# Restoring the node order of a row of attention scores with a VectorE transpose of 32x32 squares before the row goes to DRAM

## The chip, the cores and the metric

The kernel runs on one core of a Trainium2 chip. The metric is the device time of one execution in microseconds (us), the median of several runs; lower is better. The core's engines are TensorE (PE: matmuls; PEld: its weight loads), VectorE (DVE), ScalarE (ACT), GpSimd (POOL) and SyncE (SP), whose queue issues most of the DMA transfers. Each engine works through its own instructions in a fixed order and waits on semaphores for the others.

## The reference

There are 32 graphs of 512 nodes with 256 features. Each graph goes through four layers of graph attention; every layer normalises `x`, applies a ReLU, computes attention and adds the result to `x`. Layers 1 and 2 form their attention from one score per node on each side. Cut to what matters here (`B` = 32, `N` = 512):

```python
def layer_1(h, adj, W, a):                     # layer 2 is alike, with exp(-leaky_relu(.))
    Wh = h @ W.T
    src = Wh @ a[:256, 0]                      # a score for each row of the attention
    dst = Wh @ a[256:, 0]                      # a score for each column
    e = src[:, :, None] + dst[:, None, :]
    e = jnp.where(e > 0, e, 0.2 * e)           # leaky ReLU
    e = jnp.where(adj > 0, e, NEG_INF)
    return softmax(e) @ Wh

for layer in (0, 1, 2, 3):
    h = relu(layernorm(x))
    x = x + gnn[layer](h, adj)
```

Layer 0 uses dot products of the nodes, two tanh convolutions and a softmax, layer 3 a bilinear score with a leaky ReLU. The output is `x` after layer 3, as float32.

## The kernel before, in words

The work is done one graph at a time, with up to five graphs in flight (`FLIGHT = 5`, five "slots"), and for each graph in tiles of 128 nodes (`NT` = 4 tiles). Attention is kept transposed: partitions hold the columns' nodes (128 of them per tile `c`), the free dimension holds all 512 rows.

The order of instructions is made when the program is built. Each operation is registered by `op(engine, cost, after, emit, *tiles)`: `cost` is a pair of nanoseconds, how long the engine is held and when the result is there. `Plan.best` runs a list scheduler over all operations of all graphs with these prices, tries several spacings between graphs, keeps the shortest plan, and the instructions are written out in that order. The buffers (36 pages of SBUF, 8 PSUM banks, 4 value buffers, 5 slots) are handed out by this plan too. The prices are constants near the top: `A_PRELU`, `A_PRELU2`, `A_EXP` for ScalarE, `V_TINY`, `V_MASK` for VectorE, `D_OUT`, `D_SPREAD`, `D_TURN` for DMA transfers.

For layers 1 and 2 `scored_values` multiplies the nodes with a weight matrix that has two more columns (L596), so that each bank holds 256 values and two scores per node. VectorE copies the two scores of each tile into a small tile `sd` (L600), whose partition is the node within its tile and whose free dimension is the tile's number; ScalarE copies the values (L603).

`leaky_exp_t` then needs one of the two scores as a row of 512 that is the same on all 128 partitions. It has two ways. The first five and the last five graphs (`turned`) use TensorE: four transposes of a broadcast column (L619) put the row into a PSUM bank, `bank_r`. The other 22 graphs go through DRAM: `collect` (L624) writes the 128x4 scores to DRAM, partition after partition, and `spread` (L628) reads the 512 numbers back onto every partition, into the tile `row`. In this row the numbers stand in the order partition, tile; the node order is tile, partition. ScalarE therefore reads `row` with a step of four floats when it adds the other score and takes the leaky ReLU (`leaky`, L635, activation function Prelu). The exp follows (`exp`, L639), then VectorE applies the adjacency mask (L764 in layer 1, L791 in layer 2), and `attend` (L662) multiplies the attention with the values.

Other lines that are spoken of later: in layer 0, ScalarE's exp (L700), VectorE's mask (L703), the reciprocal of the softmax sum on VectorE (L711) and the tanh on ScalarE (`y`, L714), which reads an attention bank and so sets it free; in layer 3, the leaky ReLU (L924), the same activation function on consecutive floats in SBUF. The weights are loaded at the start by transfers that GpSimd issues (L289), after a few memsets.

Of the kernel before, what the change touches and what calls it, by code (L numbers as in the profile page):

```python
# [11 lines left out]
F32 = mybir.dt.float32  # L12
# [3 lines left out]
AF = mybir.ActivationFunctionType  # L16
# [3 lines left out]
P = 128  # L20
EPS = 1e-5
ALPHA = 0.2
# [17 lines left out]
A_COPY, A_HALF, A_PRELU, A_EXP, A_TANH = (477.0, 597.0), (253.0, 373.0), (570.0, 693.0), (519.0, 640.0), (373.0, 474.0)  # L40
A_BIAS, A_PRELU2 = (570.0, 687.0), (629.0, 722.0)
# [2 lines left out]
A_HALF_BIAS = (345.0, 460.0)  # L44
A_NORM, A_JOIN, V_SPLIT = (491.0, 590.0), (620.0, 767.0), (332.0, 422.0)
D_TURN = (1310.0, 2600.0)
D_OUT, D_SPREAD = (550.0, 3500.0), (550.0, 4500.0)
D_X, D_ADJ, D_ADJ0 = (550.0, 5000.0), (550.0, 12000.0), (550.0, 2500.0)
G_LOAD = (800.0, 5000.0)

# [108 lines left out]
def kernel(  # L159
# [31 lines left out]
    nc = tc.nc  # L191
    B, N, H = x.shape
    NT = N // P
    HC = H // P
    HALF = H // 2
    FLIGHT = 5
    PAGES, VALUES = 36, 4
    LEAD = 2

    const = ctx.enter_context(tc.tile_pool(name="const", bufs=1))  # L200
    work = ctx.enter_context(tc.tile_pool(name="work", bufs=1))
    ps = ctx.enter_context(tc.tile_pool(name="ps", bufs=1, space=PSUM))
    dram = ctx.enter_context(tc.tile_pool(name="dram", bufs=2, space=bass.MemoryType.DRAM))


    cols, pair, stat, turned = [P, HC, N], [P, NT, H], [P, NT], [P, NT, N]
# [8 lines left out]
        "code": (turned, BF16, "code"), "adj": (turned, I32, "adj"),  # L215
        "planes": ([P, 2, H], U16, "planes"), "planesT": ([P, 2 * HC, P], U16, "planesT"),
        "bank": ([P, 512], F32, "bank"), "v": (None, F32, "v"),
        "st": ([P, NT, 6], F32, None), "mv": ([P, NT, 2], F32, None), "sd": ([P, 2, NT], F32, None),
        "ve": (stat, F32, None), "rstd": (stat, F32, None), "rs": (stat, F32, None), "off": (stat, F32, None),
        "top": (stat, BF16, None),  # L220
    }
    POOLS = {"page": PAGES, "v": VALUES, "code": 1, "adj": 1, "planes": 3, "planesT": 2, "bank": 8,
             "slot": FLIGHT, "ahead": FLIGHT + 1}

    plan = Plan()
# [1 line left out]
    class Tiles:  # L227
# [10 lines left out]
        def place(self, key):  # L238
            if key not in self.places:
                self.places[key] = plan.place(key if key in POOLS else KINDS[self.kind(key)][2])  # L240
            return self.places[key]
# [22 lines left out]
    ident = const.tile([P, P], F32, tag="ident", name="ident")  # L264
# [72 lines left out]
    def seven_of(w, dst, half, after, *keys):  # L337


        def blocks():  # L340
# [29 lines left out]
    a = [load(l1_sb, rows_of(l1_w), "raw0")]  # L370
# [4 lines left out]
    a = [load(l2_aug[:, :, :H], rows_of(l2_w))]  # L375
    a = ready["l2"] = a + transposed(lambda: l2_aug[:, :, :H], l2_wt, a, "raw1")
    a = a + [load_column(l2_ac, l2_a.rearrange("o n -> (o n)"))]
# [3 lines left out]
    t = transposed(l3_sb, wt3, [load(l3_sb, rows_of(l3_w), "raw2")], "raw2", "raw4")  # L381
    a = product(lambda d: awt()[:, d, :], a12_sb, lambda c: wt3()[:, c, :], H,
                t + [load(a12_sb, rows_of(l3_a12), "raw3")], "raw3", "raw4", "raw5")
    a = product(lambda d: m3_sb()[:, d, :], wt3, lambda c: awt()[:, c, :], H, a, "raw4", "raw5", "raw6")
# [4 lines left out]
    a = [load(lambda i=i: l3_wide()[:, :, i * (HALF + 1) : i * (HALF + 1) + HALF],  # L389
              rows_of(l3_w2)[:, :, i * HALF : (i + 1) * HALF], "raw8") for i in range(2)]  # L390
# [8 lines left out]
    for i in range(VALUES):  # L399
        v = const.tile([P, NT, LEAD + H + 1], F32, tag=f"v{i}", name=f"v{i}")  # L400
        nc.gpsimd.memset(v[:, :, LEAD + H :], 1.0)
        v_bufs.append(v)


    def graph(b, adj_before, x_before):


        T = Tiles(b)

        def op(engine, cost, after, emit, *keys):  # L410
            return plan.op(engine, cost, after, emit, b, T.uses(keys))
# [10 lines left out]
        def e(l, c):  # L422

            return T[f"e{l}_{c // 2}"][:, c % 2, :]
# [20 lines left out]
        coded, code = [], None  # L445
        for g in range(NT // 2):
            code = op("V", V_CODE, [got_adj[2 * g + 2], code], partial(classes, g), "adj", "code", "slot")
# [107 lines left out]
        def block_sums(dst, source, b, after, left):  # L555
# [24 lines left out]
            else:  # L580
# [2 lines left out]
            return (lambda x: [sums[x][0]] if x in sums else list(after),  # L583
                    lambda x: d(sums[x][1]) if x in sums else b(*plain[x]))

        def scored_values(l, hs, w_aug, ready):


            cols = w_aug.shape[2]
            vs, ss = [], []  # L590
            for t in range(NT):
                key = f"bank_v{l}{t}"

                def product(t, key):
                    for c in range(HC):
                        nc.tensor.matmul(T[key][:, :cols], T[f"hT{l}"][:, c, t * P : (t + 1) * P],  # L596
                                         w_aug[:, c, :], start=(c == 0), stop=(c == HC - 1))

                def scores(t, key):
                    nc.vector.tensor_copy(T[f"sd{l}"][:, : cols - H, t], T[key][:, H:cols])  # L600

                def values(t, key):
                    nc.scalar.copy(T[f"v{l}"][:, t, LEAD : LEAD + H], T[key][:, :H])  # L603

                a = op("PE", pe(n256=4), [hs[t]] + ready, partial(product, t, key), key, f"hT{l}")
                ss.append(op("V", V_TINY, [a], partial(scores, t, key), key))
                vs.append(op("A", A_HALF, [a], partial(values, t, key), key, f"v{l}"))
            return vs, ss

        def leaky_exp_t(l, ss, sign):  # L610

            turned = b < FLIGHT or b >= B - FLIGHT
            key = f"bank_r{l}" if turned else f"row{l}"
            line = []

            def turn(t):
                nc.tensor.transpose(T[key][:, t * P : (t + 1) * P],  # L619
                                    T[f"sd{l}"][:, 0, t : t + 1].to_broadcast([P, P]), ident)  # L620

            def collect():
                line.append(dram.tile([P, NT], F32, tag=f"row_{T.places['slot']['number']}", name=f"row{l}_{b}"))
                nc.sync.dma_start(out=line[0], in_=T[f"sd{l}"][:, 0, :])  # L624

            def spread():
                d = line[0]
                nc.sync.dma_start(out=T[key][:, 0, :], in_=bass.AP(tensor=d.tensor, offset=d.offset, ap=[[0, P], [1, N]]))  # L628

            def leaky(c):  # L630
                if turned:
                    row = T[key].rearrange("q (t p) -> q t p", t=NT)
                else:
                    row = T[key][:, 0, :].rearrange("q (p t) -> q t p", t=NT)
                nc.scalar.activation(e(l, c).rearrange("q (t p) -> q t p", t=NT), row, AF.Prelu,  # L635
                                     bias=T[f"sd{l}"][:, 1, c : c + 1], alpha=ALPHA)

            def exp(c):
                nc.scalar.activation(e(l, c), e(l, c), AF.Exp, scale=sign)  # L639

            a = None
            if turned:
                for t in range(NT):
                    a = op("PE", pe(nt=1), [ss[t], a], partial(turn, t), key)
            else:
                a = op("D", D_OUT, ss, collect)
                a = op("D", D_SPREAD, [a], spread, key)
            ls = [op("A", A_PRELU, [a], partial(leaky, c), key, f"e{l}_{c // 2}") for c in range(NT)]
            return [op("A", A_EXP, [x], partial(exp, c), f"e{l}_{c // 2}") for c, x in enumerate(ls)]

        def attend(l, es, vs, use):
# [23 lines left out]
        for g in range(NT // 2):  # L675
            key = f"bank_v0{g}"
# [11 lines left out]
            a = op("PE", pe(n256=8), hs[two(g)], partial(values, g, key), key, "hT0")  # L688
            vs += [op("V", V_ADD, [a], partial(biased_v, g, j, key), key, "v0") for j in range(2)]
        es = []  # L690
        for c in range(NT):
            key = f"bank_q{c}"
# [12 lines left out]
            a = op("PE", pe(n512=4), qs, partial(similar, c, key), key, "hT0", "fa0")  # L705
            a = op("A", A_COPY, [a], partial(exp0, c, key), key, f"e0_{c // 2}")
# [22 lines left out]
        a = None  # L729
        for c in range(NT):  # L730
            a = op("PE", pe(n512=4), [ys[c], a], partial(again, c), "bank_z0", "bank_z1", "y0", f"e0_{c // 2}")
        zs = [op("A", A_COPY, [a], partial(evacuate_z, k), f"bank_z{k}", "zT") for k in range(HC)]
        xs = []
        for g in range(NT // 2):
            key = f"bank_o{g}"
# [18 lines left out]
            a = op("PE", pe(n256=8), zs + ready["w1"], partial(second_conv, g, key), key, "zT")  # L754
            bs = [op("V", V_PSUM, [a] + ready["b1"], partial(biased, 2 * g + j, key), key, "z0") for j in range(2)]
            a = op("A", A_EXP, bs, partial(tanh2, g), "z0")
# [11 lines left out]
        vs, ss = scored_values(1, hs, l1_aug, ready["l1"])  # L768
# [18 lines left out]
        vs, ss = scored_values(2, hs, l2_aug, ready["l2"])  # L787
# [109 lines left out]
        ls = [(sb[c // 2, 0], sb[c // 2, 1]) for c in range(NT)]  # L897
# [35 lines left out]
        a = op("V", (334.0, 425.0), hi, highest, "crest3")  # L933
        a = op("D", D_TURN, [a], partial(turn, 0, 2), "crest3")
        a = op("V", (900.0, 1000.0), [a], tops, "crest3")
        a = op("D", D_TURN, [a], partial(turn, 1, 0), "crest3")
        row = op("A", A_PRELU2, [a], leaky_row, "crest3")
        ls = [op("A", A_PRELU2, [a, hi[c // 2]], partial(leaky3, c), f"e3_{c // 2}") for c, a in enumerate(ls)]
        ls = [op("V", V_MASK, [a, row], partial(shifted, c), "crest3", f"e3_{c // 2}") for c, a in enumerate(ls)]
# [41 lines left out]
        for g in range(NT // 2):  # L981
            u = op("V", V_MASK, us[two(g)], partial(upper3, g), "y3", "x")
            l = op("A", A_BIAS, us[two(g)], partial(exp4, g), "y3", "r3")
# [8 lines left out]
    code, got_x = None, None  # L992
    for b in range(B):
        code, got_x = graph(b, code, got_x)
# [37 lines left out]
```

The softmax here doesn't subtract the row's maximum and nothing guards it: scores larger than these inputs give would overflow.

## Time and profile before

| what | value |
|---|---|
| time, median of 3 runs | 2461.58 us (2461.34 to 2461.85) |
| span of the profiled execution | 2459.7 us |
| PE busy | 2407.4 us, 98% |
| DVE busy | 1876.2 us, 76% |
| ACT busy | 1742.8 us, 71% |
| POOL busy | 253.8 us, 10% |
| DMA `row<-sd` (collect) | 44 transfers of 2 KB, median 3.2 us from issue to landing |
| DMA `row<-row` (spread) | 44 transfers of 256 KB, median 3.7 us |
| score copies `sd<-bank_v` on DVE | 256, mean 157 ns |

"Busy" is the time in which at least one instruction of the engine was recorded as running. In a group of instructions the columns are: line, engine, operation, output and inputs by their names in the program, shapes, count, then total busy time and mean time of one, then the idle time of the engine just before these instructions and what ended it. In a timeline or chain the columns are start, length, and what ran; a bracket says how long the engine had been idle and which instruction released it. In the list of waits they are: total, number of times, longest. A matmul is pipelined: its record overlaps that of the next.

### The profile page before, as it was taken

How to read it: one execution, taken by the hardware profiler on the slowest of the kernel's cores; microseconds unless marked ns; L12 is line 12 of the kernel's file. 1: busy time of each engine (PE TensorE's matmuls, PEld its weight loads, DVE VectorE, ACT ScalarE, POOL GpSimd, SP SyncE). 2: the span in 40 equal slices, each digit the busy share in tenths (PEclk: the TensorE clock that was granted, in tenths of full speed). 3: DMA queues.
4: the chain of work that ended last, by engine and by line, in shares of the span. 5: the costliest groups of instructions: out<-in, count | busy, mean ns of one | idle time of the engine just before them, and what ended most of it. 6: DMA issues, size and time to landing. Idle time of an engine off the chain costs nothing.

```text
span 2459.7 us, 33966 instructions
## 1 busy us (share of the span) xinstructions
PE 2407.4 (98%) x10700; PEld 1877.3 (76%) x10700; DVE 1876.2 (76%) x5733; ACT 1742.8 (71%) x3233; POOL 253.8 (10%) x315
## 2 busy tenths in 40 slices
PE   7999999999999999999999999999999999999998
PEld 4678777777777777777777777777777777777877
DVE  5468878777777877787777777777777778756888
ACT  4466777767777777777677777777776777755884
POOL 2001001110010101011101101010011011100110
PEclk9999999999999999999999999999999999999999
DMA  7223333332333322333323333233333343321221
GB/s 178 46 56 82 73 69 82 82 74 54 80 76 82 82 64 64 80 80 82 71 54 81 74 82 82 64 65 80 80 76 70 62 83 81 71 46 22 44 46 41
DMA packets 437204, 175.92 MB, mean 72 GB/s; under 512 B 393408, under 2 KB 410432, under 8 KB 437024
## 3 DMA queue, kind: packets, MB, share of 16 engines
q1 hardware_dynamic: 430976, 154.34, 29.9%
q0 software_dynamic: 5360, 18.75, 2.3%
q8 instruction: 85, 1.39, 0.2%
q14 instruction: 95, 0.78, 0.1%
q10 hardware_dynamic: 688, 0.66, 0.1%
HBM read 64.49 MB, written 16.87 MB: 33 GB/s over the span
## 4 chain that ended last, share of the span: by engine, by line
PE 73%; ACT 17%; DVE 5%; issue 3%; DMA 2%; POOL 0%; SPq 0%; POOLq 0%; ACTq 0%; DVEq 0%
PE bank_a L662 28%; PE bank_v L596 9%; PE bank_z L723 9%; ACT e L635 8%; PE bank_o L741 4%; PE bank_f L513 4%; PE bank_f L838 4%; PE bank_w L855 4%; ACT e L639 3%; PE bank_q L696 3%; PE bank_v L855 3%; PE bank_s L878 3%; ACT xn L475 2%; PE bank_v L682 2%; ACT e L700 1%
## 5 line engine op out<-in xcount | busy, mean ns | idle before, releaser
L662 PE MATMUL bank_a<-v,e 128*128 128x257 f32 (+1 forms) x4096 | 978.0, 381 | 21.8 <-ACT y L714 17.5
L662 PEld LDWEIGHTS bank_a<-v,e 128*128 128x128 f32 x4096 | 757.9, 190 | 199.9 <-issue 68.6
L488 ACT COPY hT<-planesT 128x512 uint16<-128x512 uint16 x512 | 383.2, 767 | 42.1 <-DMA planesT<-planes 41.7
L468 POOL TENSOR_TENSOR rstd<-ve,mhalf 128x2 f32<-128x2 f32 x256 | 215.2, 849 | 1891.7 <-DVE ve L465 1807.6
L475 ACT ACTIVATE xn<-x,off,rstd 128x256 f32<-128x256 f32 x512 | 277.3, 593 | 123.1 <-DVE off L471 119.3
L596 PE MATMUL bank_v<-l_aug,hT 128*128 128x258 f32 x1024 | 251.5, 383 | 3.3 <-ACT r L807 1.7
L480 DVE COPY planes<-xn 128x512 uint16<-128x512 uint16 x512 | 207.9, 422 | 43.8 <-ACT xn L475 24.1
L723 PE MATMUL bank_z<-e,y 128*128 128x512 f32 x512 | 240.6, 592 | 0.0
L696 PE MATMUL bank_q<-fa,hT 128*128 128x512 f32 x512 | 239.3, 592 | 0.0
L596 PEld LDWEIGHTS bank_v<-l_aug,hT 128*128 128x128 f32 x1024 | 192.2, 191 | 35.5 <-issue 3.6
L461 DVE BATCH_NORM_STATS2 st<-x 128x6 f32<-128x256 f32 x512 | 209.0, 408 | 6.6 <-DMA x<-in_x_dram 6.6
L635 ACT ACTIVATE e<-row,sd 128x512 f32<-128x512 f32 x176 | 207.0, 1229 | 0.0
L603 ACT COPY v<-bank_v 128x256 f32<-128x256 f32 x256 | 92.9, 375 | 90.1 <-PE bank_v L596 75.8
L639 ACT ACTIVATE e<-e 128x512 f32<-128x512 f32 x256 | 151.9, 632 | 0.0
L696 PEld LDWEIGHTS bank_q<-fa,hT 128*128 128x128 f32 x512 | 94.9, 190 | 71.4 <-issue 60.8
L723 PEld LDWEIGHTS bank_z<-e,y 128*128 128x128 f32 x512 | 96.5, 190 | 69.1 <-issue 57.9
L885 DVE SCALAR_TENSOR_TENSOR e<-bank_s,v,mask 128x256 f32<-128x256 f32 x256 | 111.1, 476 | 16.5 <-PE bank_s L878 16.3
L682 PE MATMUL bank_v<-w_sb,hT 128*128 128x256 f32 x512 | 121.4, 380 | 0.0
L703 DVE TENSOR_TENSOR e<-e,mask 128x512 f32<-128x512 f32 x128 | 87.5, 688 | 44.0 <-ACT e L700 43.9
L741 PE MATMUL bank_o<-w_sb,zT 128*128 128x256 f32 x512 | 120.4, 379 | 0.0
L513 PE MATMUL bank_f<-hT,att_sb 128*128 128x512 f32 x256 | 119.8, 593 | 0.0
L682 PEld LDWEIGHTS bank_v<-w_sb,hT 128*128 128x128 f32 x512 | 97.1, 191 | 23.9 <-issue 6.1
(134 smaller groups left out, 3702.1 us busy)
## 6 DMA issues: line engine op xcount, KB each, us to landing
adj<-in_adj_dram SPq DMA_DIRECT2D x128, 256.0 KB, 2.9
x<-in_x_dram SPq DMA_DIRECT2D x32, 512.0 KB, 5.1
out_dram<-y POOLq DMA_DIRECT2D x32, 512.0 KB, 4.1
row<-row SPq DMA_DIRECT2D x44, 256.0 KB, 3.7
planesT<-planes SPq DMA_TRANSPOSE x512, 2.4
codeT<-code SPq DMA_TRANSPOSE x128, 2.6
crest<-crest SPq DMA_TRANSPOSE x64, 2.4
raw_w<-in_L_gnn_W_dram POOLq DMA_DIRECT2D x3, 256.0 KB, 7.1
```

Source lines behind the costliest of these rows:

```text
L468: nc.gpsimd.tensor_tensor(T[f"rstd{l}"][:, two(g)], T[f"ve{l}"][:, two(g)], mhalf[:, two(g)], ALU.pow)
L475: nc.scalar.activation(T[f"xn{l}"][:, t, :], T["x"][:, t, :], AF.Relu, bias=T[f"off{l}"][:, t : t + 1], scale=T[f"rstd{l}"][:, t : t + 1])
L488: nc.scalar.copy(bits[:, :, :, t * P : (t + 1) * P], T[f"planesT{l}_{t}"].rearrange("p (b c) n -> p b c n", b=2))
L513: nc.tensor.matmul(T[key], w_sb[:, c, k * P : (k + 1) * P], T[f"hT{l}"][:, c, :], start=(c == 0), stop=(c == HC - 1))
L596: nc.tensor.matmul(T[key][:, :cols], T[f"hT{l}"][:, c, t * P : (t + 1) * P], w_aug[:, c, :], start=(c == 0), stop=(c == HC - 1))
L635: nc.scalar.activation(e(l, c).rearrange("q (t p) -> q t p", t=NT), row, AF.Prelu, bias=T[f"sd{l}"][:, 1, c : c + 1], alpha=ALPHA)
L639: nc.scalar.activation(e(l, c), e(l, c), AF.Exp, scale=sign)
L662: nc.tensor.matmul(T[keys[j]][:, : LEAD + H + 1 - lead], e(l, c)[:, t * P : (t + 1) * P], T[f"v{l}"][:, c, lead:], start=(c == 0), stop=(c ...
L682: nc.tensor.matmul(T[key][:, j * H : (j + 1) * H], T["hT0"][:, c, t * P : (t + 1) * P], w0_sb[:, c, :], start=(c == 0), stop=(c == HC - 1))
L696: nc.tensor.matmul(T[key], T["hT0"][:, k, c * P : (c + 1) * P], T["fa0"][:, k, :], start=(k == 0), stop=(k == HC - 1))
L723: nc.tensor.matmul(T[f"bank_z{k}"], T["y0"][:, c, k * P : (k + 1) * P], e(0, c), start=(c == 0), stop=(c == NT - 1))
L741: nc.tensor.matmul(T[key][:, j * H : (j + 1) * H], T["zT"][:, k, t * P : (t + 1) * P], w1_sb[:, k, :], start=(k == 0), stop=(k == HC - 1))
```

## The change

The change brings the row into node order before it goes to DRAM, so that ScalarE can read it as consecutive floats.

- The scores of a slot live in one tile of 128 x 132 floats that is zeroed once by GpSimd. VectorE's copy for tile `t` puts the row's score into column `32 * t` and the other score into column `128 + t`. The slice with the step `P - 31 * t` names just these two columns.
- A new VectorE instruction, `squares`, transposes the 128x128 part in squares of 32x32 into a tile `sT` (pool of two). The column at the left edge of each square becomes its top row, so partitions 0, 32, 64 and 96 of `sT` hold the scores, 32 consecutive nodes per square.
- `collect` writes these four partitions, 16 pieces of 32 floats, to DRAM in node order. `spread` is as before.
- `leaky` reads the row, or the PSUM bank, as it stands.
- The prices for the planner: a new one for the transpose, a lower one for the landing of `collect`, and `A_PRELU2` in place of `A_PRELU` for the leaky ReLU on the row from DRAM. `A_PRELU2` is (629, 722) ns, `A_PRELU` (570, 693) ns.

The graphs that use TensorE for the row keep doing so, with the scores in the new tile.

```diff
+V_SQUARES = (180.0, 270.0)
-D_OUT, D_SPREAD = (550.0, 3500.0), (550.0, 4500.0)
+D_OUT, D_SPREAD = (550.0, 2500.0), (550.0, 4500.0)
...
-        "st": ..., "mv": ..., "sd": ([P, 2, NT], F32, None),
+        "st": ..., "mv": ..., "sT": ([P, P], F32, "sT"),
...
+    for i in range(FLIGHT):
+        s = const.tile([P, P + NT], F32, tag=f"scores{i}", name=f"scores{i}")
+        nc.gpsimd.memset(s, 0.0)
+        score_bufs.append(s)
...
                 def scores(t, key):
-                    nc.vector.tensor_copy(T[f"sd{l}"][:, : cols - H, t], T[key][:, H:cols])
+                    nc.vector.tensor_copy(scores_of()[:, 32 * t : P + 1 + t : P - 31 * t], T[key][:, H:cols])
...
             def turn(t):
                 nc.tensor.transpose(T[key][:, t * P : (t + 1) * P],
-                                    T[f"sd{l}"][:, 0, t : t + 1].to_broadcast([P, P]), ident)
+                                    scores_of()[:, 32 * t : 32 * t + 1].to_broadcast([P, P]), ident)
+
+            def squares():
+                nc.vector.transpose(T[f"sT{l}"], scores_of()[:, :P])
 
             def collect():
-                line.append(dram.tile([P, NT], F32, ...))
-                nc.sync.dma_start(out=line[0], in_=T[f"sd{l}"][:, 0, :])
+                line.append(dram.tile([N], F32, ...))
+                nc.sync.dma_start(out=line[0].rearrange("(t g j) -> g t j", t=NT, j=32),
+                                  in_=T[f"sT{l}"][0:P:32, :].rearrange("g (t j) -> g t j", t=NT))
...
             def leaky(c):
-                if turned:
-                    row = T[key].rearrange("q (t p) -> q t p", t=NT)
-                else:
-                    row = T[key][:, 0, :].rearrange("q (p t) -> q t p", t=NT)
-                nc.scalar.activation(e(l, c).rearrange("q (t p) -> q t p", t=NT), row, AF.Prelu,
-                                     bias=T[f"sd{l}"][:, 1, c : c + 1], alpha=ALPHA)
+                row = T[key] if turned else T[key][:, 0, :]
+                nc.scalar.activation(e(l, c), row, AF.Prelu, bias=scores_of()[:, P + c : P + c + 1], alpha=ALPHA)
...
-                a = op("D", D_OUT, ss, collect)
+                a = op("V", V_SQUARES, ss, squares, f"sT{l}")
+                a = op("D", D_OUT, [a], collect, f"sT{l}")
                 a = op("D", D_SPREAD, [a], spread, key)
-            ls = [op("A", A_PRELU, [a], partial(leaky, c), ...) for c in range(NT)]
+            ls = [op("A", A_PRELU if turned else A_PRELU2, [a], partial(leaky, c), ...) for c in range(NT)]
```

## The prediction, made before the changed kernel ran

> **What bounds the kernel now.** I read the page first (busy shares), then who waited for whom on TensorE, then the timeline of TensorE and VectorE over one graph, then the chain of waits over the same stretch, and last the groups of instructions kept apart by shape.
>
> The page and the list of TensorE's waits:
>
> ```profile
> PE 2407.4 (98%) x10700; PEld 1877.3 (76%) x10700; DVE 1876.2 (76%) x5733; ACT 1742.8 (71%) x3233; POOL 253.8 (10%) x315
> ...
> PE bank_a L662 <- ACT y L714: 17.5, 20, 0.9
> PE bank_w L309 <- DMA raw_w<-in_L_gnn_W_dram: 11.2, 1, 11.2
> PE bank_w L326 <- DVE raw_w L312: 4.8, 2, 3.6
> PE bank_v L596 <- ACT r L807: 1.7, 1, 1.7
> ```
>
> TensorE works 98% of the span, and its longest wait in total is one of 0.9 us that comes 20 times: for `y` of layer 0 on ScalarE (L714), which must read a PSUM bank before the matmuls of L662 go on. In the timeline of TensorE it is one hole in each graph's turn:
>
> ```profile
> 1091.99 6.66 PE L662 MATMUL bank_a<-v,e 128*128 128x257 f32 x30
> 1099.55 4.17 PE L662 MATMUL bank_a<-v,e 128*128 128x257 f32 x18 [0.90 <-ACT y L714]
> ```
>
> The 16 matmuls of L596 with which the chain enters each turn start at 1059.67 and again at 1135.00, so a turn takes 75.33 us. A matmul of L662 is recorded as 381 ns, but 20 of them in a row take 4.33 us in the chain of waits, 0.217 each: 0.165 us of each lies under the next one. The hole therefore costs 0.90 + 0.165, some 1.06 us, and the other 74.3 us are packed. Outside these holes TensorE loses the first 11.2 us, 4.8 us of waits at the start, some 9 us of small waits after 2290 us, and the store at the end.
>
> What makes `y` late is in the chain of waits before the hole, and in VectorE's timeline:
>
> ```profile
> 1077.33 2.24 ACT e L635 x2
> ...
> 1081.09 2.25 ACT e L635 x2
> ...
> 1086.14 2.22 ACT e L635 x2
> ...
> 1089.88 2.26 ACT e L635 x2
> 1092.13 0.53 ACT e L639
> 1092.66 0.02 issue
> 1092.68 0.69 DVE e L764
> ```
>
> ```profile
> 1092.68 0.69 DVE L764 TENSOR_TENSOR e<-e,mask 128x512 f32<-128x512 f32 x1 [1.26 <-ACT e L639]
> ...
> 1098.14 0.23 DVE L711 RECIPROCAL rs<-bank_a 128x1 f32<-128x1 f32 x2
> ```
>
> Between 1077.3 and 1092.1 us eight leaky-ReLUs of the score rows (L635) stand in ScalarE's queue, 1.12 us apiece. VectorE idles 1.26 us for the exp behind them and is then busy without a break until the reciprocal L711, which releases `y`. So ScalarE's L635 sets the hole, though ScalarE is busy only 71%. The groups by shape show why L635 is long:
>
> ```profile
> L635 ACT ACTIVATE e<-row,sd 128x512 f32<-128x512 f32 x176 | 207.0, 1229 | 0.0
> L635 ACT ACTIVATE e<-bank_r,sd 128x512 f32<-128x512 f32 x80 | 52.4, 693 | 14.0 <-PE bank_r L619 13.9
> L924 ACT ACTIVATE e<-e,zero 128x512 f32<-128x512 f32 x128 | 85.3, 716 | 30.9 <-DVE crest L902 30.8
> ```
>
> The same function on 512 consecutive floats takes 716 ns from SBUF (L924) and 693 from PSUM; from `row`, read 16 bytes apart, 1229.
>
> **What the Trainium skill says.** "SBUF — State Buffer", section "Door 1: The DMA port swizzle", says that SBUF gives full speed to accesses that stay in one 16-byte line and that each access to a new line pays; four floats is one line. The row is read with a step of four floats, each access in a new line: the trace agrees, 1229 against 716 ns. "ScalarE: Activation LUTs", section "What ACT_TABLE_LOAD costs", gives an activation with a pointer bias about 280 ns + 0.833 ns per element, 93 ns of it under the next; for 512 that is 707 and 614 ns. L924 shows 716 ns, which agrees. "DMA: Bandwidth & Descriptors", section "Why a DMA increments its semaphore by 16 and not by 1", says that the engines used must divide the outermost sizes of both sides: the new transfer, of 4 partitions, would run on 4 engines, the old one of 128 partitions on 16. No trace shows the new one yet.
>
> **The change part by part.** 22 of the 32 graphs (all but the first and last five) send their row through DRAM, for layers 1 and 2.
>
> *Removed: the strided read.* From 1.12 us of ScalarE's time to some 0.62 (716 ns less the overlap of 93): 0.50 us × 8 = 4.0 us in each of these graphs, 176 × 0.50 = 88 us in all. On the path to the end counts only what fills the hole: 1.06 us of the 4.0. Between the rows and `y` nothing else gets longer, so the hole closes with about 3 us to spare. The planner also now books this step at 629 ns, not 570, so its order no longer rests on a price half of the true one. Gain: 20 holes × (17.5 / 20 + 0.165) = 20.8 us. The rest of the 88 us is hidden behind packed matmuls.
>
> *Added: VectorE's transpose of 128x128 floats*, two per such graph, 44 in all. The trace has none. From below: a 128x128 copy at L343 took 221 ns; from above: "VectorE: DVE Perf Modes", section "The three transpose paths", gives 311 ns for 128x128 in bf16. I take 0.25 us: 44 × 0.25 = 11 us of VectorE, 0.5 us per turn (bounds 0.44 and 0.62), where it works about 59 of 75 us (48 of 61 us in a slice of the span). The transpose waits for the four score copies, which the collecting transfer waited for before; queued behind it on VectorE are masks and norm statistics, late by 0.25 us at most, and VectorE idled 1.26 us for ScalarE anyway. Cost on the path: 0.
>
> *Changed: the transfer to DRAM.* 128 pieces of 16 bytes become 16 of 128 bytes. Before it took 3.2 us (median) from issue to landing; with fewer pieces on fewer engines I expect 2 to 3.5. The spread (3.7 us) stays. It and the transposes of `planes` are queued behind on SyncE; the built order still has the collecting transfer among them, with other transfers between it and its spread, so a difference below 1 us moves ScalarE's start on the row, which then has 4 us less to do. Cost: 0.
>
> *Moved: scores kept in one zeroed tile per slot.* Five memsets of 128x132 on GpSimd stand before the weights' transfers; `ident`'s 128x128 took 204 ns, so up to 1.0 us, of which I count 0.3 at the start, as they overlap in part (+0.3). In the built order, VectorE's small score copies wait for ScalarE's copy of the same bank in 151 of 176 cases, not 88; such waits cost 33.9 us over 75 before, 0.45 each, so 63 more are 28 us of VectorE, 1.3 us in each of 22 turns.
>
> *Re-planned.* The planner reorders everything. The matmuls are the same in number and shape apart from the names, and a turn in the built order holds the same matmuls as before.
>
> Sum: 2461.6 − 20.8 + 0.3 = 2441.1 us.
>
> **The rivals.** (1) *The hole stays at half.* The extra waits of the score copies (1.3 us) and the transposes (0.5 us) make VectorE 1.8 us later per turn. What ScalarE gives back is 4.0 us, so this should not use it up, but the new order may put them just ahead of the reciprocals. Half of 20.8: 2451. (2) *Hidden anyway.* If `y` is late because VectorE's queue ahead of L711 is simply long (5.5 us without a break from 1092.68), a faster ScalarE does nothing: about 2461. Against it: the queue began after a wait of 1.26 us for ScalarE, and another of 1.54 us shortly before. (3) *Slower.* A new wait in the repeated turn. If the row comes later on SyncE's queue, or the new order leaves a second hole, half of today's size beyond today's in each of 22 turns, that is 22 × 0.5 = 11 us: about 2472. For it: the built order leaves 20 us of matmuls, not 30, between layer 2's scores and the first matmuls on its attention. Against it: a shorter transfer and 2 us less ScalarE work per layer. (4) *More than the holes.* The waits after 2290 us, 9 us in sum, and the long matmuls after them shrink with a better order: about 2434.
>
> **How the numbers follow.** Forecast 55%; (4) 12%; (1) 15%; (2) 8%; (3) 10%. Faster is forecast, (4) and (1): 82%; same is (2): 8%; slower is (3): 10%. The time is the forecast's, 2441. The range runs from 2432, a little below (4), to 2460, the edge of (2): it leaves out (3), most of (2), and little of (4).
>
> **What would show it.** Right: the row form of L635 near 716 ns; no wait of TensorE for `y` of layer 0 repeated in every turn; a turn of 74.3 us; ScalarE busy about 88 us less; VectorE's busy time up by about 11 us; the transfer landing in under 3.5 us. Wrong: a row form above 900 ns; a repeated wait of TensorE of 0.5 us or more on another line; a span that shrinks while the turn stays at 75.3 us, which would put the gain at the ends and not in the holes.

## The result and the profile after

The changed kernel took 2437.61 us (median of 4 runs) against 2461.46 us for the kernel before in the same comparison: ratio 0.9902, 95% interval 0.9885 to 0.9919, that is 23.9 us less. A later comparison of the same pair gave 0.9898 (0.9885 to 0.9912). The forecast was 2441 us, in a range of 2432 to 2460.

Two lines of the changed kernel's page (busy times, and the shares of the chain that ended last), and the second of these as the kernel before had it:

```profile
PE 2404.1 (99%) x10700; PEld 1880.8 (77%) x10700; DVE 1879.5 (77%) x5777; ACT 1674.6 (69%) x3233; POOL 250.0 (10%) x320
PE 94%; issue 3%; DMA 2%; ACT 1%; DVE 0%; POOL 0%; SPq 0%; POOLq 0%; DVEq 0%
```

```profile
PE 73%; ACT 17%; DVE 5%; issue 3%; DMA 2%; POOL 0%; SPq 0%; POOLq 0%; ACTq 0%; DVEq 0%
```

The chain is now TensorE to 94%; before it was 73%, with 17% of ScalarE. TensorE's waits in the stretch from 500 to 2000 us, where the turns repeat, first before, then after (columns: what waited, for what, total us, times, longest):

```profile
PE bank_a L662 <- ACT y L714: 16.6, 19, 0.9
```

```profile
PE bank_v L607 <- ACT hT L495: 1.0, 3, 0.6
```

In these 1500 us TensorE now waits 1.0 us in all, and the wait for `y` is not there. In TensorE's timeline, the first matmuls of layer 0's attention and the convolutions that follow them (L736) now stand close:

```profile
1087.64 2.76 PE L675 MATMUL bank_a<-v,e 128*128 128x257 f32 x12
1090.24 1.88 PE L736 MATMUL bank_z<-e,y 128*128 128x512 f32 x4
1091.96 2.76 PE L675 MATMUL bank_a<-v,e 128*128 128x257 f32 x12
1094.56 1.88 PE L736 MATMUL bank_z<-e,y 128*128 128x512 f32 x4
```

No bracket stands behind any of these lines, so TensorE had not been idle. A turn can be taken from the first such convolution of one graph to that of the next. The kernel before took 75.3 us for it, and the changed one 74.16 us in most turns; over the 19 turns from the seventh graph's to the 26th's the means are 75.28 and 74.24 us.

The groups by shape, and last the line of layer 1's mask on VectorE as it was before (L764, now L777):

```profile
L648 ACT ACTIVATE e<-row,scores 128x512 f32<-128x512 f32 x176 | 118.9, 714 | 7.4 <-DMA row<-row 7.3
L937 ACT ACTIVATE e<-e,zero 128x512 f32<-128x512 f32 x128 | 83.9, 713 | 26.6 <-DVE crest L915 26.5
L777 DVE TENSOR_TENSOR e<-e,mask 128x512 f32<-128x512 f32 x128 | 86.7, 684 | 1.8 <-ACT e L651 1.8
L611 DVE COPY scores<-bank_v 128x2 f32<-128x2 f32 x256 | 40.4, 159 | 51.1 <-ACT v L614 35.2 <-PE bank_v L607 8.5
L635 DVE STREAM_TRANSPOSE sT<-scores 128x128 f32<-128x128 f32 x44 | 12.9, 292 | 0.0
```

```profile
L764 DVE TENSOR_TENSOR e<-e,mask 128x512 f32<-128x512 f32 x128 | 85.2, 687 | 33.3 <-ACT e L639 32.9
```

The leaky ReLU on the row takes 714 ns, as long as the one of layer 3 (L937), where it took 1229. Layer 1's mask on VectorE waited 33.3 us in all before, nearly all of it for ScalarE's exp, and waits 1.8 us now. ScalarE has a wait that is new, 7.3 us in all for the spread row, and VectorE's transposes take 12.9 us.

### The profile page after: what moved, and what is told of

Read it like the earlier page. It is cut to its first block, busy times and chain, and to the rows that moved or that the text cites. A ratio compares the mean times of both kernels' runs of the same rounds, so it can differ in the third digit from the quotient of the medians.

```text
span 2435.8 us, 34064 instructions
## 1 busy us (share of the span) xinstructions
PE 2404.1 (99%) x10700; PEld 1880.8 (77%) x10700; DVE 1879.5 (77%) x5777; ACT 1674.6 (69%) x3233; POOL 250.0 (10%) x320
## 2 busy tenths in 40 slices
DMA packets 431748, 175.91 MB, mean 72 GB/s; under 512 B 387952, under 2 KB 404976, under 8 KB 431568
## 4 chain that ended last, share of the span: by engine, by line
PE 94%; issue 3%; DMA 2%; ACT 1%; DVE 0%; POOL 0%; SPq 0%; POOLq 0%; DVEq 0%
PE bank_a L675 35%; PE bank_z L736 9%; PE bank_v L607 9%; PE bank_q L709 9%; PE bank_s L891 7%; PE bank_o L754 5%; PE bank_f L520 5%; PE bank_v L695 4%; PE bank_w L868 4%; PE bank_v L868 4%; PE bank_f L851 4%; DMA planesT<-planes 1%; DMA x<-in_x_dram 1%; PE bank_r L631 0%; ACT hT L495 0%
## 5 line engine op out<-in xcount | busy, mean ns | idle before, releaser
L495 ACT COPY hT<-planesT 128x512 uint16<-128x512 uint16 x512 | 372.8, 764 | 42.9 <-DMA planesT<-planes 42.1
L482 ACT ACTIVATE xn<-x,off,rstd 128x256 f32<-128x256 f32 x512 | 282.2, 595 | 72.7 <-DVE off L478 65.5
L736 PE MATMUL bank_z<-e,y 128*128 128x512 f32 x512 | 240.6, 592 | 0.0
L651 ACT ACTIVATE e<-e 128x512 f32<-128x512 f32 x256 | 153.2, 626 | 0.0
L736 PEld LDWEIGHTS bank_z<-e,y 128*128 128x128 f32 x512 | 96.7, 190 | 68.4 <-issue 60.5
L648 ACT ACTIVATE e<-row,scores 128x512 f32<-128x512 f32 x176 | 118.9, 714 | 7.4 <-DMA row<-row 7.3
L943 ACT ACTIVATE e<-e 128x512 f32<-128x512 f32 x128 | 79.6, 629 | 61.3 <-DVE e L940 60.3
L713 ACT ACTIVATE e<-bank_q 128x512 f32<-128x512 f32 x128 | 76.2, 596 | 55.7 <-PE bank_q L709 55.0
```

What stands on the lines that cost most here:

```text
L482: nc.scalar.activation(T[f"xn{l}"][:, t, :], T["x"][:, t, :], AF.Relu, bias=T[f"off{l}"][:, t : t + 1], scale=T[f"rstd{l}"][:, t : t + 1])
L495: nc.scalar.copy(bits[:, :, :, t * P : (t + 1) * P], T[f"planesT{l}_{t}"].rearrange("p (b c) n -> p b c n", b=2))
L736: nc.tensor.matmul(T[f"bank_z{k}"], T["y0"][:, c, k * P : (k + 1) * P], e(0, c), start=(c == 0), stop=(c == NT - 1))
```

## The experiments

The result alone doesn't say why the hole closed. The change did two things at once: it made ScalarE's read fast, and, through three prices, it made the planner write another order. Theory A: the fast read closed the hole. Theory B: the new order did. Ratios are to the kernel before, timed together with each of them, with 95% intervals.

**The old order with a fast read.** The same instructions in the same order on every engine as in the kernel before; the row stands in DRAM in the order partition, tile, and is read as if it were in node order, so the attention of layers 1 and 2 uses permuted scores.

```diff
-                    row = T[key][:, 0, :].rearrange("q (p t) -> q t p", t=NT)
+                    row = T[key][:, 0, :].rearrange("q (t p) -> q t p", t=NT)
```

> The kernel before, instruction for instruction in its order and with its prices, but the row is read as consecutive floats as it lies (so the scores of the row stand in the wrong node order). Theory A: the row form takes 0.71 us, the wait for y is gone, a turn takes 74.3 us, 2461.5 - 20.8 = about 2441 us. Theory B: the hole stays where the order puts it, 2457 to 2462 us.

Measured: 2441.04 us against 2463.74, ratio 0.9909 (0.9893 to 0.9926). The row form, layer 1's mask, and the only wait of TensorE listed from 500 to 2000 us:

```profile
L635 ACT ACTIVATE e<-row,sd 128x512 f32<-128x512 f32 x176 | 117.1, 716 | 0.0
L764 DVE TENSOR_TENSOR e<-e,mask 128x512 f32<-128x512 f32 x128 | 84.5, 685 | 6.1 <-ACT e L639 5.6
```

```profile
PE bank_v L596 <- ACT hT L488: 0.8, 1, 0.8
```

TensorE's wait for `y` is gone and a turn takes 74.16 us. The fast read is enough by itself, as theory A has it.

**The new order with a slow read.** The changed kernel in its order, with the transpose and the transfer, but the row read with a step of four floats (again permuted scores).

```diff
-                row = T[key] if turned else T[key][:, 0, :]
-                nc.scalar.activation(e(l, c), row, AF.Prelu, ...)
+                row = T[key].rearrange("q (t p) -> q t p", t=NT) if turned else T[key][:, 0, :].rearrange("q (p t) -> q t p", t=NT)
+                nc.scalar.activation(e(l, c).rearrange("q (t p) -> q t p", t=NT), row, AF.Prelu, ...)
```

> The changed kernel in its own order, with transpose and transfer, but the row read with a step of four floats as before (again a wrong node order). Theory A: the row form is back at 1.23 us, ScalarE is late by 4 us per graph, and TensorE waits again in each turn, 2452 to 2475 us. Theory B: the new order hides it, 2436 to 2441 us.

Measured: 2441.31 us, ratio 0.9911 (0.9897 to 0.9926). Theory A's expectation failed: the read is slow again, and the time is not.

```profile
L648 ACT ACTIVATE e<-row,scores 128x512 f32<-128x512 f32 x176 | 210.1, 1235 | 1.3 <-DMA row<-row 1.3
L777 DVE TENSOR_TENSOR e<-e,mask 128x512 f32<-128x512 f32 x128 | 86.8, 684 | 4.8 <-ACT e L651 4.8
```

```profile
PE bank_v L607 <- ACT hT L495: 1.0, 3, 0.6
PE bank_a L675 <- ACT r L820: 0.8, 1, 0.8
```

The last two are all of TensorE's waits from 500 to 2000 us. ScalarE's timeline of this kernel in one turn, and two lines of VectorE's, show how the new order bears the slow read:

```profile
1085.01 2.39 ACT L648 ACTIVATE e<-row,scores 128x512 f32<-128x512 f32 x2
1087.26 0.66 ACT L651 ACTIVATE e<-e 128x512 f32<-128x512 f32 x1
1087.78 0.50 ACT L727 ACTIVATE y<-bank_a,rs 128x256 f32<-128x256 f32 x1
1088.14 0.67 ACT L651 ACTIVATE e<-e 128x512 f32<-128x512 f32 x1
1088.65 1.27 ACT L648 ACTIVATE e<-row,scores 128x512 f32<-128x512 f32 x1
1089.79 0.49 ACT L727 ACTIVATE y<-bank_a,rs 128x256 f32<-128x256 f32 x1
```

```profile
1086.28 0.23 DVE L724 RECIPROCAL rs<-bank_a 128x1 f32<-128x1 f32 x2
1089.15 0.69 DVE L777 TENSOR_TENSOR e<-e,mask 128x512 f32<-128x512 f32 x1
```

The first two `y` (L727) stand between the rows, and on VectorE their reciprocals (L724) come before layer 1's masks (L777); in the old order both stood behind all eight rows and the masks. So each half of the change closes the hole alone, and there the two do not add up.

**Which price made the order.** Three kernels leave the read slow and change one price of the kernel before each (`A_STRIDED` is a new constant).

```diff
 e1: the leaky ReLU on the row at what it takes
-            ls = [op("A", A_PRELU, ...
+A_STRIDED = (1130.0, 1240.0)
+            ls = [op("A", A_PRELU if turned else A_STRIDED, ...
 e6: the same at the price that the changed kernel uses
+            ls = [op("A", A_PRELU if turned else A_PRELU2, ...
 e9: the collecting transfer at the price that the changed kernel uses
-D_OUT, D_SPREAD = (550.0, 3500.0), (550.0, 4500.0)
+D_OUT, D_SPREAD = (550.0, 2500.0), (550.0, 4500.0)
```

> The kernel before with one price changed: the leaky ReLU of the strided row is booked at (1130, 1240) ns, what it takes, in place of (570, 693). The read stays strided. Theory A (the fast read itself closed the hole in each turn): the row form stays near 1.23 us, some of the hole stays, over 2455 us. Theory B (the order made with a true price closed it): the wait for y is gone from the repeated turn, 2438 to 2445 us.

> The kernel before with the leaky ReLU of the strided row booked at (629, 722) ns, as the changed kernel books it, not (570, 693); the read takes 1.23 us as ever. If the hole was an accident of one order that any re-planning may undo: gone from the repeated turn, 2438 to 2447 us. If the planner has to know the true 1.13 us to hide it: still a wait in each turn, 2455 to 2466 us.

> The kernel before with one price changed: the landing of the collecting transfer booked at 2500 ns, as the changed kernel books it, not 3500. The strided read stays. If this price is what brought the order that hides the slow read: ratio to before 0.989 to 0.994. If not: the wait for y comes back each turn, 0.997 to 1.003.

Measured: with the true price 2445.6 us, ratio 0.9930 (0.9915 to 0.9945); with 629 ns 2463.57 us, ratio 0.9997 (0.9988 to 1.0005); with the transfer's price 2469.27 us, ratio 1.0020 (1.0013 to 1.0027). TensorE's waits from 500 to 2000 us, for the three in this order:

```profile
PE bank_v L597 <- ACT hT L489: 2.1, 3, 1.1
PE bank_w L856 <- DVE w L951: 0.9, 5, 0.2
```

```profile
PE bank_a L662 <- ACT y L714: 18.4, 20, 1.2
```

```profile
PE bank_a L662 <- DVE e L764: 11.4, 20, 1.3
PE bank_v L596 <- ACT hT L488: 8.0, 19, 0.7
PE bank_w L855 <- ACT y L714: 0.6, 2, 0.4
```

With the true price the holes are gone although each read still takes 1232 ns: theory B's mechanism exists, and the price is enough. It is still 0.3% over the changed kernel: its turns vary, from 73.3 to 76.0 us, and take 74.43 us on the mean against 74.24; why was not followed further. With 629 ns the same hole stands at the same place. With the cheaper transfer there are two holes in each turn in place of one, both behind late work of ScalarE (the mask L764 waits for the exp behind the rows, and `hT` stands behind rows too), a turn takes 75.6 us in most cases, and the kernel is slower than before. So planning anew does not by itself help. An order made with a price half of the true one is at the mercy of where the lateness lands: of four such orders that met the slow read, two had the hole (the kernel before and the one with 629 ns), one had two, and one, that of the changed kernel, had none.

**All of the change but its prices.** The changed kernel with `D_OUT` at 3500 ns and `A_PRELU` for the row.

```diff
-D_OUT, D_SPREAD = (550.0, 2500.0), (550.0, 4500.0)
+D_OUT, D_SPREAD = (550.0, 3500.0), (550.0, 4500.0)
-            ls = [op("A", A_PRELU if turned else A_PRELU2, ...
+            ls = [op("A", A_PRELU, ...
```

> The changed kernel with the two prices of before (3500 ns for the collecting transfer, 570 for the leaky ReLU), so all of the change but its re-pricing. If the fast read is enough under any order near the old one: ratio 0.988 to 0.992. If the gain needs the new order: over 0.994.

Measured: 2444.51 us, ratio 0.9913 (0.9898 to 0.9928). With the fast read this order, a third one, has no repeated hole either: TensorE's only wait from 500 to 2000 us is one of 0.4 us.

**A fast read booked as slow.** The changed kernel with (1130, 1240) ns for the leaky ReLU.

```diff
-            ls = [op("A", A_PRELU if turned else A_PRELU2, ...
+A_STRIDED = (1130.0, 1240.0)
+            ls = [op("A", A_PRELU if turned else A_STRIDED, ...
```

> The changed kernel with the leaky ReLU booked at (1130, 1240) ns although it takes 0.71 us. If both remedies add up: under 0.988. If the hole is the only thing either can give: 0.988 to 0.993.

Measured: 2439.23 us, ratio 0.9898 (0.9883 to 0.9913). Nothing is added. Its turns are 74.16 us too, and TensorE has no wait at all from 500 to 2000 us: it is full there, and neither remedy has more to give.

**The cost of the transpose.**

```diff
             def squares():
-                nc.vector.transpose(T[f"sT{l}"], scores_of()[:, :P])
+                for _ in range(5):
+                    nc.vector.transpose(T[f"sT{l}"], scores_of()[:, :P])
```

> The changed kernel with each transpose of squares done five times over in the same place: 176 more of some 0.24 us, 42 us more of VectorE in all, nearly 1 us more ahead of each collecting transfer. If the transpose lies beside packed matmuls: 2436 to 2442 us. If VectorE or the row's way to ScalarE is close to setting the turn: half of the 42 us or more comes through, over 2455 us.

Measured: 2441.54 us, ratio 0.9908 (0.9893 to 0.9923), which cannot be told from the changed kernel's 0.9902 or 0.9898.

```profile
L649 ACT ACTIVATE e<-row,scores 128x512 f32<-128x512 f32 x176 | 119.2, 715 | 26.1 <-DMA row<-row 26.0
L636 DVE STREAM_TRANSPOSE sT<-scores 128x128 f32<-128x128 f32 x220 | 67.7, 308 | 6.1
```

The group of transposes grew by 54.8 us, ScalarE's idle time for the row from 7.3 to 26.0 us, and the time by nothing that stands out of the noise. The turns hint at a small cost: 74.42 us on the mean, against 74.24 and 74.30 in two executions of the changed kernel, so some 0.1 to 0.2 us for eight more transposes in a turn. The rest lies beside packed matmuls.

**More rows through DRAM.** Now that ScalarE reads such a row fast, the graphs at the ends might use it too, and TensorE be spared 40 or 64 transposes. The changed kernel ran once more beside them.

```diff
-            turned = b < FLIGHT or b >= B - FLIGHT
+            turned = b >= B - FLIGHT          # e7;  e8: turned = b >= B - 2
```

> The changed kernel once more, as the measure for the others of this call: 0.990 of the kernel before, within 0.002.

> The changed kernel with the row of the first five graphs sent through DRAM too. This takes 40 transposes of 0.11 us from TensorE, 4.4 us. If TensorE alone sets the time there: 4 us less than the changed kernel. If the longer way through DRAM (some 6 us more per row) leaves TensorE waiting while few graphs are in flight: no gain, or up to 6 us more.

> The changed kernel with only the last two graphs using TensorE for the row: 64 transposes of 0.11 us fewer, 7.0 us. If TensorE alone sets the time: 7 us less than the changed kernel. If the longer way shows where the work runs out: at least 3 us more than with the first five alone.

Measured: the changed kernel 2439.95 us, 0.9898 (0.9885 to 0.9912); the first five by DRAM 2445.2 us, 0.9920 (0.9907 to 0.9932); all but two 2456.22 us, 0.9960 (0.9947 to 0.9974). TensorE's longest waits from 100 to 300 us with the first five by DRAM:

```profile
PE bank_a L675 <- DVE e L716: 4.2, 1, 4.2
PE bank_w L868 <- ACT w L959: 1.5, 2, 1.1
```

The changed kernel has no wait of TensorE in this stretch; here there are six, 7.2 us in all. From 180 to 200 us, around the longest of them, the granted clock (the share of its full clock that TensorE was given) was 0.83, against 1.00 in the changed kernel. The twelve matmuls after the longest wait took 4.3 us from start to start, some 2.1 us more than such matmuls take further on. These 9.3 us are more than the 4.4 us of matmuls saved; by the medians the kernel lost 5.2 us. With all but two by DRAM the waits in this stretch make 14.2 us, and the clock was 0.86 from 180 to 200 us and 0.83 from 220 to 240. These kernels were re-planned too, so the loss is that of the way and its order together. No version tried beats the changed kernel.

## Why the prediction was right, step by step

*TensorE's hole is the only thing to win in the repeated turn.* Right. A turn went from 75.3 to 74.16 us, and in no kernel is the median turn shorter.

*A hole costs 1.06 us, 20 of them 20.8 us.* Right. The 19 turns took 1430.3 us before and 1410.6 after, which is 1.04 us a turn, just what the sum counted (17.5 / 20 + 0.165). In the old order with the fast read the mean turn is 74.17 us, 1.11 us less than before; nothing else changed there, and it gained 2463.74 − 2441.04 = 22.7 us.

*The ends: +0.3 us.* Mis-sized, and here lie the 3.5 us by which the forecast was too long. TensorE's waits in the first 100 us went from 16.0 to 17.5 us. Those after 2290 us went from 9.0 to 3.9 us, though with the longest single wait:

```profile
PE bank_a L675 <- ACT e L943: 2.8, 1, 2.8
PE bank_v L868 <- DVE v L881: 0.9, 2, 0.7
PE bank_w L868 <- DVE w L963: 0.2, 1, 0.2
```

So 20.8 + 5.1 − 1.5 = 24.4 us of the gain can be read from TensorE's waits in the two profiled executions, against 23.9 measured. The shorter waits at the end belong to the changed kernel's order, not to the fast read: with the same order and the slow read they make 4.2 us, while the old order with the fast read and the two other orders with the fast read, under old and dear prices, have 8.2 us each. The longer wait at the start can't be put down to the five memsets: of two kernels timed together, the old order with the fast read has none of them and waited 18.8 us there, and the new order with the slow read has them and waited 18.9.

*The strided read on ScalarE makes `y` late, and 0.50 us apiece is given back.* Shown. The row form went from 1229 to 714 ns, its busy time by 88.1 us against the 88 forecast, and with this alone the hole closed. VectorE's wait for the exp fell from 33.3 to 6.1 us in the old order, so most of the wait of 1.26 us in each turn is gone; that some 3 us would be to spare is not measured. But the prediction gave the new price only half a sentence, and did not say that an order alone could have closed the hole. It could: the new order with the slow read, and the old kernel with the true price, both have no hole. So the forecast was safer than it was argued to be: two remedies worked for it where it counted one, and either alone gives about 2441 us.

*ScalarE busy 88 us less.* The group fell by that, and all groups of ScalarE together by 1918.8 − 1832.1 = 86.7 us. ScalarE as a whole, where records that overlap count once, fell by only 1742.8 − 1674.6 = 68.2 us: its records overlap less than before. That is perhaps because an activation that follows an idle gap has none ahead of it to overlap with; no run isolates that.

*The transpose costs 0.25 us each and nothing on the path.* The size was off, inside the stated bounds: 292 ns on the mean, 12.9 us for 44. That it costs next to nothing on the path is shown by five of them in place of one.

*63 more score copies wait for ScalarE, 28 us of VectorE.* Wrong. That wait rose only from 33.9 us (75 times) to 35.2 (71 times): a wait written in front of an instruction is not a wait that happens, and in most of the 256 cases VectorE did not stand idle for ScalarE's copy. VectorE's busy time rose by 3.3 us, not 11.

*The transfer lands in 2 to 3.5 us.* Open: the trace of the changed kernel has no landing times for it. The spread follows the collecting transfer after a median of 4.3 us on SyncE's queue, 5.1 before, with other transfers between them in both. The old transfer's own median went with the order: 3.2 us in the kernel before, 1.4 us in the one with the cheaper transfer. That 4 engines carry the new one in place of 16 is not shown directly. The two pages list 437204 and 431748 DMA packets, 124 fewer for each of the 44 transfers; 112 of these are the pieces (16 in place of 128), and the other 12 would fit if each engine adds one packet of its own.

*The rivals.* Half a hole and a hidden gain did not come. Of more than the holes a part came, the 5.1 us less of waits at the end. The slower one came in another kernel: with the cheaper transfer and the slow read, two smaller holes in each turn made 0.2% more.

## What to carry to other kernels

Where one engine is full, look for the hole that repeats, follow it back to the instruction that was late, and ask what the schedule believed of its duration. With the slow read, a price half of the true one gave orders from 0.9911 to 1.0020 of the kernel before, by luck; the true price alone gave 0.9930. The faster instruction gave 0.9898 to 0.9913 under four different orders of the same work. A faster step and a better order for a slow one can be two cures for one illness: test each alone before adding up their gains.

## What the runs showed of the hardware that had not been expected

VectorE's transposes of 128x128 floats took 292 ns each on the mean in the changed kernel (44 of them). Where five stood in a row they took 308 ns (220), but single ones took 304 ns in the kernel with the first five graphs by DRAM (54), so the row need not be the reason. VectorE's total busy time rose by 43.5 us for the 176 added. A 128x128 float copy took 221 ns, so the transpose in squares costs under 100 ns more than a copy of the same size.
